# Graph attention over sorted edges on one core: three one-hot tables moved behind the spreads of q for the last tile, and the next queries' first part moved ahead of a node pair's add

## The chip, the cores and the metric

The kernel runs on one core of a Trainium2 chip. The metric is device microseconds of that core from start to end of one execution, median of several runs. Before the change it is 2704.53 us, the median of 3 runs between 2700.92 and 2709.87.

## What is computed

One layer of graph attention between two layer norms, on 12,500 nodes of 256 numbers and 200,000 edges. The edges come sorted by their destination `dst`; destinations are drawn as a square, so nodes with low numbers have far more edges than those with high ones. There are 8 heads of D = 32 numbers. The reference, cut to what matters:

```python
h = maximum(layernorm(x), 0)                      # (12500, 256)
q = (h @ Wq).reshape(n, 8, 32); k = h @ Wk; v = h @ Wv      # biases are zero
logits = einsum('ehd,ehd->eh', q[dst], k[src]) / sqrt(32)   # one row an edge
expv = exp(logits - segment_max(logits, dst)[dst])
attn = expv / segment_sum(expv, dst)[dst]
agg = segment_sum(attn[:, :, None] * v[src], dst)
out = agg.reshape(n, 256) + h @ Wskip
y = h + gelu(out)
return x + layernorm(y) * gamma + beta
```

## The kernel before

A first phase (to about 300 us) computes h, writes one table of keys and values to HBM (`kv_tab`, 512 floats a node: 256 of k, 256 of v) and lays out the edges. Then `walk_streams` goes through them. The edges are cut into S = 8 streams of consecutive edges. The walk makes NST = 66 steps (loop variable c); in a step each stream moves on by K = 3 tiles (j = 0, 1, 2) of 128 edges. A tile is thus 128 edges of 8 streams at once, with an edge on each partition.

What a tile goes through, with the name of the helper and its line:

- GpSimd (POOL) gathers the rows of `kv_tab` for the tile's sources with indirect DMAs (L1340), eight a tile, one for each stream, 24 a step. They land in the tile `kv`.
- TensorE spreads the queries: the q of a window of nodes (`qw`) times a one-hot table (`to_e`) gives each edge the q of its destination. `spread` (L1385 to L1396, the matmuls L1392) does half of the streams in a call and writes a PSUM tile `ps_qe`, of which there are two.
- VectorE multiplies the gathered keys by the spread q in `times` (L1402, again in two halves) and sums over each head in `total` (L1409).
- `turn` (L1428, TensorE; copy by ScalarE L1431) transposes the logits. Once a step, `maxima` takes running maxima over equal destinations (scans on VectorE, L1440 on; exp on ScalarE), and `turn_back` (L1450) transposes the weights back.
- `weigh` (L1477) multiplies the gathered values by the weights on VectorE, and `add_up` (L1500) sums them to their nodes: a matmul with another one-hot table (`to_n`). Its third call in a step is copied out by ScalarE (L1513).

The tables for a coming step are made ahead, two steps before they are used. `turn_windows` transposes the nodes' h (L1302, copy to `hwT` by ScalarE L1306), `queries` makes q of it (bias L1316, matmuls L1320, copy to `qw` by ScalarE L1323), in a first part of one block and a second of two. `hot_e` makes a block of the one-hot table `to_e`: a matmul (L1366) and a relu by ScalarE (L1369), four blocks a step. `hot_n` (L1379, L1382) makes `to_n`. These all take their PSUM from `ps_hot`, of which there are two.

The sums of finished nodes go to a table in HBM. From step 18 on, a `Pair` is finished in each step: two blocks of 128 nodes. Its parts run over three steps. `fetch` (six loads on SP's queue), then in the next step `turn` (L1071, copied by ScalarE L1074), `divisors`, `skip` (h @ Wskip, L1088), `divide` (L1077), `add` (L1093, adds the attention's result to the skip's in PSUM by an identity matmul for each block), `gelu` (ScalarE, L1097), and at the end of the step `stats` (VectorE, L1100 to L1109) and `root` (ScalarE, L1113); then, a step later, `factors` (VectorE, L1117 and L1118), `normal` (ScalarE, L1123), `shifted` (TensorE, L1153), `scale` (L1157) and `store` (SP, L1168). In the loop, `pair` is the one in its second step, `before` the one in its third and `pair_next` the one being fetched. In the stretch that is changed a `pair` is there in steps 19 to 63 (45 of them) and none in steps 0 to 18.

The order of the work is the order of the code. `keep` ties each instruction to the one before it on the same engine, so TensorE, VectorE, ScalarE and SP run them exactly as the loop calls them. The gathers have their own rule: a list `waiting` holds the rows that may be gathered next (a tile's eight come in when its buffer was last read by `weigh`), and after each step of TensorE, `turns(latest[PE])` takes one from the list and makes it wait for that matmul. A gather is thus paced by TensorE's order. GpSimd runs nothing else in these steps.

ScalarE changes its table of functions by `table_of` (L1262), which runs a dummy activation of one number: to Gelu ahead of `divide`, to Sqrt ahead of `root`, to Exp behind it.

The changed stretch is L1691 to L1713 of the main loop.

Of the kernel before, what the change touches and what calls it, by code (L numbers as in the profile page):

```python
# [48 lines left out]
S = 8  # L49
# [937 lines left out]
def walk_streams(tc, N, HID, NST, KL, many, ident, idx, d0_row, slot_row, near, near_n, e_tab, pen_tab, h_tab,  # L987
# [240 lines left out]
    with ExitStack() as es:  # L1228
# [132 lines left out]
        def hot_e(c, i):  # L1361

            if i == 0:
                step[c]["to_e"] = hot.tile([P, S // 2, CH], F32, name="to_e")
            ps = hot_ps.tile([P, S * WN], F32, name="ps_hot")
            keep(nc.tensor.matmul(ps[:, :CH], near[:, i * P:(i + 1) * P], step[c]["et"],  # L1366
                                  start=True, stop=True))
            turns(latest[PE])
            keep(nc.scalar.activation(step[c]["to_e"][:, i, :], ps[:, :CH], AF.Relu, scale=-1.0,  # L1369
                                      bias=ones))  # L1370
# [14 lines left out]
        def spread(c, j, half):  # L1385

            g = step[c]
            ps = qe_ps.tile([P, 2, 2, HID], F32, name="ps_qe")
            for a in range(2):
                for b in range(2):  # L1390
                    r = slice(b * WN, (b + 1) * WN)
                    keep(nc.tensor.matmul(ps[:, b, a, :],  # L1392
                                          g["to_e"][r, 2 * half + a, j * P:(j + 1) * P],
                                          g["qw"][r, (half + a) * half, :], start=True, stop=True))
            g["qe", half] = ps
            turns(latest[PE])  # L1396
# [220 lines left out]
        for c in range(NST - 1):  # L1617
# [73 lines left out]
            if pair:  # L1691
                table_of(AF.Gelu)
                pair.divide()
            if pair_next:
                pair_next.fetch()
            if before:
                before.store(1)
            if pair:
                pair.add()
            if c + 2 < NST:  # L1700
                queries(c + 2, 0)
            if pair:
                pair.gelu()
            turn(c + 1, 0)
            if c + 2 < NST:
                turn_windows(c + 2, 1)
                hot_e(c + 2, 0)
                queries(c + 2, 1)
                for i in range(1, S // 2):
                    hot_e(c + 2, i)  # L1710
            for half in range(2):
                times(c + 1, 1, half)
                spread(c + 1, K - 1, half)  # L1713
            total(c + 1, 1)
            weigh(c, 1)
            gather_next(c, 1)
# [491 lines left out]
```

## Time and profile before

| | |
|---|---|
| median of 3 runs | 2704.53 us |
| the profiled execution | 2724.49 us |
| its span in the trace | 2722.4 us |
| mean granted clock of TensorE | 0.815 |
| busy TensorE (PE) | 1982.6 us, 73% |
| busy VectorE (DVE) | 1869.3 us, 69% |
| busy GpSimd (POOL) | 1620.4 us, 60% |
| busy ScalarE (ACT) | 1100.8 us, 40% |
| moved by DMA | 596.02 MB, mean 219 GB/s |

The profiled execution took 20 us more than the median. Rows of the trace have the start and the duration in us, the engine, the line, the operation, out<-in with partitions x elements, and in brackets the engine's idle time ahead of it and what ended it. PE is TensorE, DVE VectorE, ACT ScalarE, POOL GpSimd, SP the queue that issues the plain DMAs. A releaser called "remote" is one that the profile can't name. Rows of a timeline that stand for several instructions give the first one's start and the time that all took together.

### The profile page before, as it was taken

What the parts mean: (1) busy time and instruction counts of PE and PEld (TensorE: products, weight loads), DVE (VectorE), ACT (ScalarE), POOL (GpSimd) and SP (SyncE); (2) the same over time, 40 slices, a digit from 0 to 9 for tenths busy, and PEclk for the clock granted to TensorE, in tenths of its full rate; (3) what the DMA queues carried; (4) which work ended last, traced back from release to release, by engine and by line L of the source; (5) the groups of instructions that cost most, each with busy time, mean ns of one, the idle gap of its engine ahead of it and who ended that gap; (6) DMA issues with size and microseconds to landing.
All of it is one profiled execution on the core that took longest, in us unless ns stands there. A gap on an engine that the chain in (4) does not pass through costs nothing.

```text
span 2722.4 us, 36232 instructions
## 1 busy us (share of the span) xinstructions
PE 1982.6 (73%) x10159; PEld 1181.6 (43%) x10159; DVE 1869.3 (69%) x2165; ACT 1100.8 (40%) x2576; POOL 1620.4 (60%) x1741
## 2 busy tenths in 40 slices
PE   9994567677677677677766777777777777777776
PEld 4442344344444444444444444444444444444443
DVE  8872666666666667766767677776677767776776
ACT  5741222222222244444444444444444444444444
POOL 5456566666666665666556556656656666565652
PEclk9996777877777788888888887888888888888878
DMA  9786566777676777777777777777777777777773
GB/s 348 287 292 196 170 200 203 208 211 206 202 206 204 217 224 217 210 220 228 221 215 213 220 220 221 219 224 225 231 218 219 220 221 229 217 216 213 230 210 108
DMA packets 278904, 596.02 MB, mean 219 GB/s; under 512 B 53040, under 2 KB 166852, under 8 KB 275616
## 3 DMA queue, kind: packets, MB, share of 16 engines
q0 software_dynamic: 128224, 421.39, 53.5%
q1 hardware_dynamic: 148996, 170.91, 19.4%
q8 instruction: 83, 1.36, 0.2%
q10 hardware_dynamic: 1472, 1.31, 0.2%
q14 instruction: 129, 1.06, 0.1%
HBM read 510.92 MB, written 82.47 MB: 218 GB/s over the span
## 4 chain that ended last, share of the span: by engine, by line
PE 43%; another core or an unknown queue 14%; issue 13%; DVE 12%; ACT 11%; POOL 3%; DMA 2%; SPq 2%; DVEq 0%; POOLq 0%; ACTq 0%
PE ps_qe L1392 9%; PE ps_a L1088 6%; PE ps_a L1500 5%; PE ps_hot L1320 5%; ACT kv L1517 4%; DVE vw L1477 4%; PE ps_kv L340 4%; DVE kv L1402 3%; DVE L L1409 2%; PE ps_hot L1500 2%; POOL kv L1340 2%; ACT sums_w L1513 2%; ACT to_n L1382 2%; PE ps_hot L1153 2%
## 5 line engine op out<-in xcount | busy, mean ns | idle before, releaser
L1340 POOL DMA_INDIRECT kv<-kv_tab,idx x1520 | 1454.5, 957 | 926.3 <-issue 370.1
L1402 DVE TENSOR_TENSOR kv<-ps_qe,kv 128x1024 f32<-128x1024 f32 x392 | 466.6, 1219 | 587.5 <-remote 266.2
L1392 PE MATMUL ps_qe<-qw,to_e 64*128 64x256 f32 x3136 | 526.1, 476 | 216.2 <-issue 116.4
L1477 DVE TENSOR_TENSOR vw<-ps_x,kv 128x2048 f32<-128x2048 f32 x194 | 442.0, 2278 | 151.2 <-ACT vw L1466 123.7
L1392 PEld LDWEIGHTS ps_qe<-qw,to_e 64*128 64x128 f32 x3136 | 384.6, 234 | 370.8 <-issue 259.0
L1409 DVE TENSOR_REDUCE L<-kv 128x64 f32<-128x2048 f32 x196 | 447.7, 2284 | 5.1
L1323 ACT COPY qw<-ps_hot 128x256 f32<-128x256 f32 (+1 forms) x132 | 63.2, 479 | 601.6 <-PE ps_hot L1320 322.3
L1320 PE MATMUL ps_hot<-w_q,hwT 128*128 128x256 f32 x792 | 246.9, 456 | 19.2 <-ACT hwT L1306 18.8
L1500 PE MATMUL ps_a<-vw,to_n 128*32 128x264 f32 (+1 forms) x2304 | 237.0, 433 | 23.4 <-ACT kv L1517 18.3
L1320 PEld LDWEIGHTS ps_hot<-w_q,hwT 128*128 128x128 f32 x792 | 164.5, 222 | 117.7 <-issue 70.1
L1306 ACT COPY hwT<-ps_hot 128x256 f32<-128x256 f32 (+1 forms) x132 | 63.3, 480 | 360.4 <-PE ps_hot L1302 189.7
L340 PE MATMUL ps_kv<-w_kv,hT 128*128 128x512 f32 x392 | 184.5, 594 | 1.0 <-ACT hT L254 0.7
L1262 ACT ACT_TABLE_LOAD x139 | 178.3, 1283 | 2.6
L1088 PE MATMUL ps_a<-w_s,hT 128*128 128x256 f32 x360 | 167.7, 645 | 11.2 <-issue 4.8
L1379 PE MATMUL ps_hot<-near_n,et 48*128 48x384 bf16 x196 | 63.0, 376 | 143.3 <-ACT to_n L1382 139.3
L1366 PE MATMUL ps_hot<-et,near 48*128 48x384 bf16 x264 | 93.0, 353 | 91.7 <-ACT ps_x L1431 44.8
L1369 ACT ACTIVATE to_e<-ps_hot,ones 128x384 f32<-128x384 f32 x264 | 142.8, 581 | 10.4 <-PE ps_hot L1366 8.6
L1500 PEld LDWEIGHTS ps_a<-vw,to_n 128*32 128x32 f32 (+1 forms) x2304 | 95.2, 127 | 112.6 <-ACT kv L1517 39.6
L1517 ACT COPY kv<-ps_a 1x264 f32<-1x264 f32 x384 | 141.5, 368 | 6.3
L1088 PEld LDWEIGHTS ps_a<-w_s,hT 128*128 128x128 f32 x360 | 112.5, 328 | 58.7 <-issue 29.7
L1123 ACT ACTIVATE sums<-sums,nm,rstd 128x256 f32<-128x256 f32 x90 | 49.1, 592 | 211.0 <-DVE nm L1118 120.5
L1513 ACT COPY sums_w<-ps_a 128x264 f32<-128x264 f32 x128 | 48.4, 378 | 202.1 <-remote 74.7
(327 smaller groups left out, 2334.6 us busy)
## 6 DMA issues: line engine op xcount, KB each, us to landing
kv<-kv_tab,idx POOLq DMA_INDIRECT x1568
kv_tab<-kvo SPq DMA_DIRECT2D x23, 1024.0 KB
hw<-h_tab SPq DMA_DIRECT2D x264, 64.0 KB
table<-sums_w SPq DMA_DIRECT2D x260, 61.9 KB
pen<-pen_tab SPq DMA_DIRECT2D x66, 192.5 KB
sums<-table SPq DMA_DIRECT2D x92, 132.0 KB
x_in<-in_x_dram SPq DMA_DIRECT2D x23, 512.0 KB
h_tab<-h SPq DMA_DIRECT2D x23, 512.0 KB
```

The source lines that it names most:

```text
L340: nc.tensor.matmul(ps_kv, hT[:, c, :], w_kv[:, c, :], start=c == 0, stop=c == KC - 1)
L1088: self.keep(nc.tensor.matmul(self.ps[:, b, :], self.hT[:, b, c, :], w_s[:, c, :], start=False, stop=False, skip_group_check=True))
L1262: keep(nc.scalar.activation(dummy[:, 1:2], dummy[:, 0:1], function))
L1320: keep(nc.tensor.matmul(ps[:, b, :], g["hwT"][:, b, k, :], w_q[:, k, :], start=False, stop=k == KC - 1, skip_group_check=True))
L1340: ins = nc.gpsimd.indirect_dma_start(out=t[:, s, :], out_offset=None, in_=kv_tab[:, :], in_offset=bass.IndirectOffsetOnAxis(ap=idx[:, s, j ...
L1369: keep(nc.scalar.activation(step[c]["to_e"][:, i, :], ps[:, :CH], AF.Relu, scale=-1.0, bias=ones))
L1392: keep(nc.tensor.matmul(ps[:, b, a, :], g["to_e"][r, 2 * half + a, j * P:(j + 1) * P], g["qw"][r, (half + a) * half, :], start=True, stop= ...
L1402: keep(nc.vector.tensor_tensor(k, g["qe", half].rearrange("p b a d -> p a b d"), k, op=OP.mult))
L1409: keep(nc.vector.tensor_reduce(g["L"][:, j, :].rearrange("p (s h) -> p s h", s=S), g["kv"][j][:, :, :HID].rearrange("p s (h d) -> p s h d" ...
L1477: keep(engine.tensor_tensor(t[:, :, HEADS:].rearrange("p s (h d) -> p s h d", h=HEADS), wj[:, :, :, None].to_broadcast([P, t.shape[1], HEA ...
L1500: keep(nc.tensor.matmul(ps[at:at + w, :], g["to_n"][:, j, i * P + at:i * P + at + w], g["vw"][j][:, s, :], start=j == 0, stop=j == tiles_o ...
L1517: keep(copy(step[c + 1]["kv"][0][0:1, s, HID - HEADS:], ps[at:at + 1, :]))
```

## The change

Only the order of calls within one step of the walk changes; no call is added or taken away.

```diff
--- before.py
+++ after.py
@@ -1691,26 +1691,27 @@
             if pair:
                 table_of(AF.Gelu)
                 pair.divide()
+            if before:
+                before.store(1)
             if pair_next:
                 pair_next.fetch()
-            if before:
-                before.store(1)
-            if pair:
-                pair.add()
             if c + 2 < NST:
                 queries(c + 2, 0)
             if pair:
-                pair.gelu()
+                pair.add()
             turn(c + 1, 0)
             if c + 2 < NST:
                 turn_windows(c + 2, 1)
                 hot_e(c + 2, 0)
                 queries(c + 2, 1)
-                for i in range(1, S // 2):
-                    hot_e(c + 2, i)
+            if pair:
+                pair.gelu()
             for half in range(2):
                 times(c + 1, 1, half)
                 spread(c + 1, K - 1, half)
+            if c + 2 < NST:
+                for i in range(1, S // 2):
+                    hot_e(c + 2, i)
             total(c + 1, 1)
             weigh(c, 1)
             gather_next(c, 1)
```

On TensorE, ahead of the changed calls stand the spreads of the second tile (L1392). Then the pair's add (L1093) and the first part of the queries (L1316, L1320) change places. Before:

```order
L1392 MATMUL ps_qe<-qw,to_e 128x256 x8
L1093 MATMUL ps_a<-o,ident 128x256 x2
L1316 LDWEIGHTS one_row
L1316 MATMUL ps_hot<-b_q_70,one_row 128x256
L1320 MATMUL ps_hot<-w_q,hwT 128x256 x2
L1428 MATMUL ps_x<-ident,L 64x128
L1302 MATMUL ps_hot<-ident,hw 128x128 x4
```

With the change:

```order
L1392 MATMUL ps_qe<-qw,to_e 128x256 x8
L1316 LDWEIGHTS one_row
L1316 MATMUL ps_hot<-b_q_70,one_row 128x256
L1320 MATMUL ps_hot<-w_q,hwT 128x256 x2
L1093 MATMUL ps_a<-o,ident 128x256 x2
L1428 MATMUL ps_x<-ident,L 64x128
L1302 MATMUL ps_hot<-ident,hw 128x128 x4
```

The add now stands between the first part of the queries and the transpose of the logits (L1428).

A little further on TensorE, behind the queries' second part, stand the one-hot tables (L1366) and the spreads of the step's last tile. Before:

```order
L1320 MATMUL ps_hot_12845<-w_q_68,hwT_12838 128x256 x4
L1366 LDWEIGHTS near_84
L1366 MATMUL ps_hot_12853<-et_12592,near_84 128x384
L1366 LDWEIGHTS near_84
L1366 MATMUL ps_hot_12857<-et_12592,near_84 128x384
L1366 LDWEIGHTS near_84
L1366 MATMUL ps_hot_12861<-et_12592,near_84 128x384
L1392 MATMUL ps_qe_12865<-qw_12519,to_e_12538 128x256 x4
L1392 MATMUL ps_qe_12871<-qw_12519,to_e_12538 128x256 x4
L1428 MATMUL ps_x_2267<-ident_62,L_12790 64x128
```

With the change:

```order
L1320 MATMUL ps_hot_12844<-w_q_68,hwT_12837 128x256 x4
L1392 MATMUL ps_qe_12854<-qw_12517,to_e_12537 128x256 x4
L1392 MATMUL ps_qe_12861<-qw_12517,to_e_12537 128x256 x4
L1366 LDWEIGHTS near_84
L1366 MATMUL ps_hot_12867<-et_12592,near_84 128x384
L1366 LDWEIGHTS near_84
L1366 MATMUL ps_hot_12870<-et_12592,near_84 128x384
L1366 LDWEIGHTS near_84
L1366 MATMUL ps_hot_12873<-et_12592,near_84 128x384
L1428 MATMUL ps_x_2267<-ident_62,L_12790 64x128
```

Both halves of the spread now stand ahead of the three tables. Since each of these calls takes one waiting gather, the seventh and eighth gather of the tile in turn, which were tied to the first two of these three tables, are now tied to the two halves of the spread. GpSimd's own order is the same, and so is VectorE's.

On ScalarE the pair's gelu (L1097) moves. Before, from the load of the Gelu table to the relu of the last three one-hot blocks:

```order
L1262 ACTIVATE dummy<-dummy 1x1
L1323 COPY qw<-ps_hot 128x256
L1097 ACTIVATE sums<-ps_a 128x512
L1431 COPY ps_x<-M 64x1
L1306 COPY hwT<-ps_hot 128x512
L1369 ACTIVATE to_e<-ps_hot,ones 128x384
L1323 COPY qw<-ps_hot 128x512
L1369 ACTIVATE to_e<-ps_hot,ones 128x384 x3
```

With the change:

```order
L1262 ACTIVATE dummy<-dummy 1x1
L1323 COPY qw<-ps_hot 128x256
L1431 COPY ps_x<-M 64x1
L1306 COPY hwT<-ps_hot 128x512
L1369 ACTIVATE to_e<-ps_hot,ones 128x384
L1323 COPY qw<-ps_hot 128x512
L1097 ACTIVATE sums<-ps_a 128x512
L1369 ACTIVATE to_e<-ps_hot,ones 128x384 x3
```

The gelu now stands behind the copies of the transposed logits, of `hwT` and of the queries' second part, and still ahead of the three relus, behind which come the load of the Sqrt table and the pair's root. On SP's queue, the store of the second block of `before` goes ahead of the six loads of `pair_next`.

## Prediction

> **What bounds the kernel now.** I read the page first, then the table of what VectorE waited for, then the timeline of one step. From the page, its first line and the chain that ended last by engine:
>
> ```profile
> span 2722.4 us, 36232 instructions
> PE 43%; another core or an unknown queue 14%; issue 13%; DVE 12%; ACT 11%; POOL 3%; DMA 2%; SPq 2%; DVEq 0%; POOLq 0%; ACTq 0%
> ```
>
> No engine fills the span, and 14% of the chain goes to releasers that the profile cannot name ("another core" cannot be: there is one). VectorE's waits (line, releaser, us in total, times, longest) say where:
>
> ```profile
> DVE kv L1402 <- remote: 266.2, 63, 34.2
> DVE kv L1402 <- PE ps_qe L1392: 208.6, 69, 9.0
> ```
>
> L1402 multiplies the gathered keys by the spread queries, L1392 is the spread. The dominant wait is thus for spreads, with half of it unnamed. The scan L1440 runs once a step, so it gives the step's length (start, duration):
>
> ```profile
> 991.90 0.95 DVE L1440 TENSOR_TENSOR_SCAN ps_x<-pen,ps_x 64x384 f32<-64x384 f32 x1
> ...
> 2626.68 0.95 DVE L1440 TENSOR_TENSOR_SCAN ps_x<-pen,ps_x 64x384 f32<-64x384 f32 x1
> ```
>
> These are the scans of steps 20 and 63, all with a node pair to finish: (2626.68 - 991.90)/43 = 38.0 us a step. By the code the reordered stretch runs with a pair in 45 steps (c = 19 to 63) and without one in 19 (c = 0 to 18). One step with a pair, four engines together, in order of time:
>
> ```profile
> 1046.57 1.13 PE L1093 MATMUL ps_a<-o,ident 128*128 128x256 f32 x4
> 1047.31 0.95 POOL L1340 DMA_INDIRECT kv<-kv_tab,idx  x1 [0.30 <-issue]
> 1049.24 0.94 POOL L1340 DMA_INDIRECT kv<-kv_tab,idx  x1 [0.98 <-PE ps_x L1428]
> 1049.28 0.60 ACT L1097 ACTIVATE sums<-ps_a 128x512 f32<-128x512 f32 x1
> 1049.85 0.59 ACT L1306 COPY hwT<-ps_hot 128x512 f32<-128x512 f32 x1
> 1050.49 0.37 PE L1316 MATMUL ps_hot<-b_q,one_row 3*128 3x512 bf16 x1 [0.70 <-ACT ps_x L1431]
> 1050.79 1.99 PE L1320 MATMUL ps_hot<-w_q,hwT 128*128 128x256 f32 x8
> 1052.61 0.68 DVE L1100 TENSOR_TENSOR sums<-sums,h 128x512 f32<-128x512 f32 x1
> 1053.30 1.57 ACT L1369 ACTIVATE to_e<-ps_hot,ones 128x384 f32<-128x384 f32 x3
> 1053.94 0.32 PE L1366 MATMUL ps_hot<-et,near 48*128 48x384 bf16 x1 [0.16 <-issue]
> 1053.95 2.04 PE L1392 MATMUL ps_qe<-qw,to_e 64*128 64x256 f32 x16
> 1054.42 0.95 POOL L1340 DMA_INDIRECT kv<-kv_tab,idx  x1 [0.30 <-issue]
> 1054.89 1.28 ACT L1262 ACT_TABLE_LOAD   x1
> 1056.30 0.28 ACT L1113 ACTIVATE rstd<-mv,eps 128x2 f32<-128x2 f32 x1
> 1058.18 0.95 POOL L1340 DMA_INDIRECT kv<-kv_tab,idx  x1 [0.31 <-issue]
> 1060.20 2.35 DVE L1402 TENSOR_TENSOR kv<-ps_qe,kv 128x1024 f32<-128x1024 f32 x2 [5.90 <-remote]
> 1061.28 0.94 POOL L1340 DMA_INDIRECT kv<-kv_tab,idx  x1 [2.16 <-remote]
> 1062.47 0.15 DVE L1117 RECIPROCAL rstd<-rstd 128x2 f32<-128x2 f32 x1
> ```
>
> VectorE idles 5.90 us before the last tile's multiplies at 1060.20, although TensorE's records put their spreads at 1053.95 to 1055.99. So TensorE's answer reaches VectorE more than 4 us after its record ends, and GpSimd's next gather (1061.28) waits for TensorE too, unnamed as well. What holds the answer? GpSimd issued gathers back to back from 1049.24 to 1058.18 + 0.95 = 1059.13, and the answer came 1.07 us after it had run out of gathers that may start. A second place in the step looks the same: ScalarE waits for the last add_up.
>
> ```profile
> 1072.70 0.95 POOL L1340 DMA_INDIRECT kv<-kv_tab,idx  x1 [0.30 <-issue]
> 1074.74 0.38 ACT L1513 COPY sums_w<-ps_a 128x264 f32<-128x264 f32 x1 [3.13 <-remote]
> ```
>
> Here the answer comes 1.09 us after the last gather's 1073.65. And one step in which GpSimd paused by chance for 2.12 us just before the spreads:
>
> ```profile
> 2154.47 0.94 POOL L1340 DMA_INDIRECT kv<-kv_tab,idx  x1 [2.12 <-issue]
> 2157.48 1.23 DVE L1402 TENSOR_TENSOR kv<-ps_qe,kv 128x1024 f32<-128x1024 f32 x1 [1.02 <-PE ps_qe L1392]
> ```
>
> There the first multiply waited only 1.02 us, with the spread named as its releaser. My reading: a long run of gathers holds back TensorE's answers. It rests on coincidence in time, so the rivals keep weight.
>
> **The change part by part.** Nothing is added or removed; VectorE's and GpSimd's orders stay.
>
> TensorE: the next queries' first part goes ahead of the older pair's add (1.06 us from 1046.57), so its answer comes about 1.06 us sooner. ScalarE: the gelu (0.60 at 1049.28) leaves its place ahead of the hwT copy, which can begin some 0.3 us sooner; the queries' second part waited 0.70 us for that copy, so it ends near 1052.4, not 1052.78. Three one-hot tables (the last is the row at 1053.94) no longer stand ahead of the spreads: these begin near 1052.4 instead of 1053.95, **1.55 us sooner**, and by their record (2.04 for both halves) the first half is done at 1053.4.
>
> Gathers: each is tied to a step of TensorE's order, one per call. Gathers 7 and 8 of the next step's first tile were tied to one-hot tables 1 and 2; they are now tied to the two halves of the spread. GpSimd's run starts 0.68 us sooner (the gather after 1047.31 may follow at 48.56, not 49.24), its sixth gather (1054.42) ends at 55.37 - 0.68 = 54.7, and the seventh may not start before the first half is answered. If the run holds the answer, the run now ends itself: answer at 54.7 + 1.07 = 55.8 instead of 1060.2.
>
> What is late next is ScalarE. Tables 1 to 3 now stand behind the spreads, and ScalarE's relu of them, the Sqrt table load and the older pair's root behind those: relu 0.58, table 3's matmul 0.32 (two banks), relus to 1.71, load 1.28, the dummy 0.13 (from the load's end, 1056.17, to the root at 1056.30), root 0.28, about 3.5 us after the answer. VectorE's reciprocal (L1117) waits for the root in order. At 55.8 + 3.5 = 59.3 it stands 3.2 us ahead of 1062.47. If instead the first half is answered at once and only the second held, one gather later (1.25), it is 60.5: 1.95 sooner. I take the middle, **2.6 us a step**: 45 x 2.6 = 117 us.
>
> The gelu behind the queries' second copy makes VectorE's stats (1052.61) about 1 us later, ending near 55.4; that lies in the 5.90 us of idle time and costs nothing unless the answer is at 53.4, when it sets the multiplies' start. The store of the finished pair's second block goes ahead of the six fetches on SP: one issue of 0.36 us from the row
>
> ```profile
> 1046.72 0.36 SPq L1168 DMA_DIRECT2D out_dram<-o  x1
> ```
>
> The fetched rows are used a step later, so I take 0; bounds -16 to +16 us (45 x 0.36).
>
> Steps without a pair:
>
> ```profile
> 691.93 1.23 DVE L1402 TENSOR_TENSOR kv<-ps_qe,kv 128x1024 f32<-128x1024 f32 x1 [2.40 <-PE ps_qe L1392]
> 696.20 1.23 DVE L1402 TENSOR_TENSOR kv<-ps_qe,kv 128x1024 f32<-128x1024 f32 x1 [3.04 <-PE ps_qe L1392]
> 696.46 0.94 POOL L1340 DMA_INDIRECT kv<-kv_tab,idx  x1 [1.98 <-PE ps_qe L1392]
> ```
>
> Only the second half is held. Its hold could shrink by all of 3.04 us, but GpSimd is back at the next tile at about 695.8 instead of 696.46, and the later holds follow GpSimd. Between 0 and 3.0 I take 0.7, GpSimd's row: 19 x 0.7 = 13 us.
>
> Sum: 117 + 13 = **130 us** less. The profiled execution took 2724.49 us (span 2722.4), 20 us above the median of the runs, 2704.53. Taken from the median: **2575 us**.
>
> **The clock, and a rule that says more.** The other wait of each step, ahead of the next tile's spreads, has the pair's skip matmuls in it, and these run slowly. First an idle time and the matmuls behind it, with the clock share (third number from the end) there and where the queries ran; then a step with less idle time:
>
> ```profile
> 1038.88 0.47 PE L1379 MATMUL ps_hot<-near_n,et 48*128 48x384 bf16 x1 [4.04 <-ACT to_n L1382]
> 1041.14 3.57 PE L1088 MATMUL ps_a<-w_s,hT 128*128 128x256 f32 x8
> ```
> ```profile
> 1040.00:1042.00 2.00, 1.86 (x6) 0.94 (x5) 1.67 (x1) 1.78 (x5) 1.70 (x2) 0.50 0.85 261
> 1050.00:1052.00 2.00, 1.51 (x7) 1.08 (x7) 2.00 (x2) 0.91 (x2) 1.39 (x3) 1.00 0.93 264
> ```
> ```profile
> 1689.86 0.48 PE L1379 MATMUL ps_hot<-near_n,et 48*128 48x384 bf16 x1 [0.94 <-ACT to_n L1382]
> 1692.12 3.78 PE L1088 MATMUL ps_a<-w_s,hT 128*128 128x256 f32 x8
> ```
>
> Eight records of this shape take 3.57 us at a share of 0.50 and 1.99 at 1.00 (L1320, 1050.79). Were the share 1.00 here, 1.6 us a step would go. The row at 1692.12 speaks against it: a single idle time of 0.94 did not bring it back. I leave it out of the sum and price it as a rival. The Trainium skill (TensorE: Matmul & The Clock Gate, "Part 1: The HAM clock gate") says that an idle window of about 3.4 us halves the clock and as much busy time restores it; by that rule 4.04 us of idle time lies just above the border, and a hold shorter by 0.7 us would bring the full clock.
>
> **The rivals.**
> - *The hold is not GpSimd's and ends when it does now (slower).* Then the answer stays at 1060.2, and tables 1 to 3, which were done before the hold, stand in it. The root comes at 60.2 + 3.5 = 63.7, and VectorE's reciprocal, 62.47 now, waits 1.2 us in every step with a pair: +54 us, **2759**. It turns slower from an answer later than 59.0. For it: at 1060.20 and 1074.74 many things end together. Against it: the pause at 2154.47.
> - *The hold has a fixed length behind its spread (small gain).* Answer at 60.2 - 1.55 = 58.65, reciprocal at 62.15: 0.3 x 45 = 14 us, and up to 1.3 x 19 = 25 where no root follows: 2665 to 2690, **2680**. This is also the case in which the change does nothing that can be told from noise.
> - *The hold goes altogether (larger gain).* Multiplies at 55.4, reciprocal near 58.3: 4.2 x 45 + 3.0 x 19 = 246 us, **2459**.
> - *The forecast, and the clock stays up behind the other hold.* 117 + 13 + 1.6 x 45 = 202 us, **2503**. Only if the earlier answers shorten that idle time too.
>
> **How the numbers follow.** Forecast 2575: 0.42. Slower rival: 0.28. Fixed hold: 0.20, of which 0.12 above a gain of 0.3% and 0.08 within (0.3%, 8 us, is about what a measurement tells from no change). Hold gone: 0.05. Clock up: 0.05. Both signs are likely: the forecast's own range runs from 2704.5 - 45 x 3.2 - 19 x 3.0 = 2504 to 2704.5 - 45 x 1.95 = 2617. The whole range reaches the slower rival with 5 us around it: 2504 to 2764. Faster 0.64, same 0.08, slower 0.28.
>
> **What would show it.** Right: the idle time before the last tile's first multiply falls from 5.9 to about 2 us, the reciprocal (L1117 in the old numbering) waits for the root, GpSimd shows a gap before its seventh gather, and steps with a pair take about 35.4 us. Wrong: that idle time stays near 5 to 6 us and the reciprocal waits over 1 us behind it (slower rival), or the steps keep 38 us because the second hold, before the copy of the last sums, grows by what the first one lost.

## The result and the profile after

The changed kernel takes 2719.03 us (median of 7 runs, 2713.68 to 2721.82), the kernel before 2704.53 (7 runs, 2697.60 to 2709.87): a ratio of 1.0058, 95% interval 1.0044 to 1.0071. It is 0.6% **slower**, where 2575 was forecast. The profiled execution took 2720.00 us, 1 us from its median; that of the kernel before, 2724.49, stood 20 us above its own. So the two traces put the changed kernel 4.5 us ahead, where the medians put it 14.5 behind: the traces can show where waits moved, but their totals can't stand for the loss.

The page, first line and chain by engine:

```profile
span 2717.9 us, 36189 instructions
PE 38%; another core or an unknown queue 15%; DVE 14%; issue 14%; ACT 13%; POOL 2%; DMA 2%; SPq 1%; POOLq 0%; DVEq 0%; ACTq 0%
```

The unnamed part is about as large as it was (14%). VectorE's waits (line, releaser, us in total, times, longest), of the changed kernel and then one row of the kernel before:

```profile
DVE vw L1477 <- ACT vw L1466: 243.9, 61, 7.2
DVE kv L1402 <- PE ps_qe L1392: 180.6, 52, 6.9
DVE kv L1402 <- remote: 103.5, 33, 29.8
DVE sums L1100 <- issue: 76.8, 34, 3.3
...
DVE sums L1100 <- ACT qw L1323: 23.1, 8, 3.4
DVE rstd L1117 <- issue: 17.2, 14, 2.5
```
```profile
DVE vw L1477 <- ACT vw L1466: 123.7, 52, 5.8
```

The wait for spreads fell: its two rows from 266.2 + 208.6 = 474.8 us to 284.1, 191 less. But the wait ahead of the weighing of the first tile (L1477) grew by 120, and about 117 us in these rows stand in places where VectorE did not wait before: ahead of the pair's stats (L1100, 76.8 + 23.1) and of the reciprocal (L1117, 17.2). These are the largest rows only. All of VectorE's idle time in the steps with a pair, added up from the rows of each trace over the 44 steps from the first pair's to the last pair's, in us a step (`e2_gelu_back_3`, the change without the gelu's move, is described below):

| VectorE idle ahead of | before | after | `e2_gelu_back_3` |
|---|---|---|---|
| the last tile's multiplies (L1402) | 5.84 | 0.86 | 0.98 |
| the pair's stats (L1100) | 0 | 2.36 | 0 |
| the reciprocal (L1117) | 0 | 0.67 | 1.68 |
| the weighing of the first tile (L1477) | 1.96 | 3.18 | 4.54 |
| the second tile's multiplies (L1402) | 2.90 | 3.35 | 3.04 |
| everything | 11.06 | 10.78 | 10.61 |

**The wait that the change went for is nearly gone, and almost all of it stands elsewhere.** The two scans that were used for the step:

```profile
990.99 0.95 DVE L1440 TENSOR_TENSOR_SCAN ps_x<-pen,ps_x 64x384 f32<-64x384 f32 x1
...
2624.84 0.95 DVE L1440 TENSOR_TENSOR_SCAN ps_x<-pen,ps_x 64x384 f32<-64x384 f32 x1
```

(2624.84 - 990.99)/43 = 38.0 us a step, as before. In the steps without a pair, the scans of steps 1 and 18, first before, then after the change:

```profile
310.72 0.96 DVE L1440 TENSOR_TENSOR_SCAN ps_x<-pen,ps_x 64x384 f32<-64x384 f32 x1 [0.52 <-PE ps_x L1428]
...
916.80 0.96 DVE L1440 TENSOR_TENSOR_SCAN ps_x<-pen,ps_x 64x384 f32<-64x384 f32 x1 [0.39 <-PE ps_x L1428]
```
```profile
305.75 0.96 DVE L1440 TENSOR_TENSOR_SCAN ps_x<-pen,ps_x 64x384 f32<-64x384 f32 x1 [1.89 <-PE ps_x L1428]
...
917.27 0.96 DVE L1440 TENSOR_TENSOR_SCAN ps_x<-pen,ps_x 64x384 f32<-64x384 f32 x1 [1.99 <-PE ps_a L1500]
```

That is 606.1 us before and 611.5 after: these 17 steps got 5.4 us longer, 0.3 a step, where 0.7 a step less was forecast. One step of the changed kernel, in order of time:

```profile
1045.79 2.35 DVE L1402 TENSOR_TENSOR kv<-ps_qe,kv 128x1024 f32<-128x1024 f32 x2 [3.16 <-PE ps_qe L1392]
...
1050.25 1.99 PE L1320 MATMUL ps_hot<-w_q,hwT 128*128 128x256 f32 x8
...
1052.30 0.95 POOL L1340 DMA_INDIRECT kv<-kv_tab,idx  x1 [0.31 <-issue]
...
1054.53 0.58 ACT L1323 COPY qw<-ps_hot 128x512 f32<-128x512 f32 x1 [4.15 <-PE ps_hot L1366]
1054.77 0.95 POOL L1340 DMA_INDIRECT kv<-kv_tab,idx  x1 [1.52 <-PE ps_hot L1366]
1055.02 0.60 ACT L1097 ACTIVATE sums<-ps_a 128x512 f32<-128x512 f32 x1
...
1055.65 0.69 DVE L1100 TENSOR_TENSOR sums<-sums,h 128x512 f32<-128x512 f32 x1 [2.99 <-issue]
...
1056.03 1.14 POOL L1340 DMA_INDIRECT kv<-kv_tab,idx  x1 [0.30 <-issue]
...
1057.37 2.36 DVE L1402 TENSOR_TENSOR kv<-ps_qe,kv 128x1024 f32<-128x1024 f32 x2
...
1059.64 0.16 DVE L1117 RECIPROCAL rstd<-rstd 128x2 f32<-128x2 f32 x1
...
1065.70 0.95 DVE L1440 TENSOR_TENSOR_SCAN ps_x<-pen,ps_x 64x384 f32<-64x384 f32 x1
...
1071.49 0.38 ACT L1513 COPY sums_w<-ps_hot 128x264 f32<-128x264 f32 x1 [4.27 <-remote]
...
1076.92 2.29 DVE L1477 TENSOR_TENSOR vw<-ps_x,kv 128x2048 f32<-128x2048 f32 x1 [3.71 <-ACT vw L1466]
...
1083.22 2.36 DVE L1402 TENSOR_TENSOR kv<-ps_qe,kv 128x1024 f32<-128x1024 f32 x2 [3.27 <-PE ps_qe L1392]
```

By chance this step begins at the same time as the one that the prediction shows: 1045.79 against 1045.82. So the two can be laid side by side. The kernel before goes on from there like this:

```profile
1045.82 2.35 DVE L1402 TENSOR_TENSOR kv<-ps_qe,kv 128x1024 f32<-128x1024 f32 x2 [2.47 <-PE ps_qe L1392]
...
1068.53 0.95 DVE L1440 TENSOR_TENSOR_SCAN ps_x<-pen,ps_x 64x384 f32<-64x384 f32 x1
...
1077.89 2.29 DVE L1477 TENSOR_TENSOR vw<-ps_x,kv 128x2048 f32<-128x2048 f32 x1 [1.87 <-ACT vw L1466]
...
1083.37 2.35 DVE L1402 TENSOR_TENSOR kv<-ps_qe,kv 128x1024 f32<-128x1024 f32 x2 [2.46 <-PE ps_qe L1392]
```

The last tile's multiplies come 2.83 us sooner (1057.37 against 1060.20), the reciprocal 2.83 (1059.64 against 1062.47), the scan 2.83 (1065.70 against 1068.53). Then the second copy of the sums (from `ps_hot`) waits 4.27 us, where in the kernel before it was the third (from `ps_a`) that waited, 3.13; the weighing is only 0.97 us sooner, and the next step's multiplies 0.15. So in this step the gain was there in the middle, and was given back before the end. Over the 44 steps, VectorE's idle time from the stats to the reciprocal shrank by 5.84 - 0.86 - 2.36 - 0.67 = 1.95 us a step, less than the 2.6 of the forecast, and the two waits behind took 1.22 + 0.45 of it.

### The profile page after: what moved, and what is told of

Read it like the earlier page. It is cut to its first block, busy times and chain, and to the rows that moved or that the text cites. A ratio compares the mean times of both kernels' runs of the same rounds, so it can differ in the third digit from the quotient of the medians.

```text
span 2717.9 us, 36189 instructions
## 1 busy us (share of the span) xinstructions
PE 1927.9 (71%) x10159; PEld 1165.6 (43%) x10159; DVE 1873.5 (69%) x2165; ACT 1111.0 (41%) x2576; POOL 1621.1 (60%) x1741
## 4 chain that ended last, share of the span: by engine, by line
PE 38%; another core or an unknown queue 15%; DVE 14%; issue 14%; ACT 13%; POOL 2%; DMA 2%; SPq 1%; POOLq 0%; DVEq 0%; ACTq 0%
PE ps_qe L1392 9%; PE ps_a L1088 6%; ACT kv L1517 6%; DVE vw L1477 5%; PE ps_hot L1320 5%; PE ps_kv L340 4%; DVE L L1409 3%; PE ps_a L1500 3%; ACT sums_w L1513 2%; DVE kv L1402 2%; PE ps_hot L1071 2%; ACT to_n L1382 2%; PE ps_hot L1379 1%; POOL kv L1340 1%
## 5 line engine op out<-in xcount | busy, mean ns | idle before, releaser
L1402 DVE TENSOR_TENSOR kv<-ps_qe,kv 128x1024 f32<-128x1024 f32 x392 | 462.9, 1218 | 337.6 <-PE ps_qe L1392 180.6
L1477 DVE TENSOR_TENSOR vw<-ps_x,kv 128x2048 f32<-128x2048 f32 x194 | 442.1, 2279 | 255.4 <-ACT vw L1466 243.9
L1392 PE MATMUL ps_qe<-qw,to_e 64*128 64x256 f32 x3136 | 511.7, 476 | 19.2 <-issue 17.4
L1392 PEld LDWEIGHTS ps_qe<-qw,to_e 64*128 64x128 f32 x3136 | 377.7, 241 | 209.3 <-issue 150.5
L1320 PE MATMUL ps_hot<-w_q,hwT 128*128 128x256 f32 x792 | 244.9, 453 | 18.5 <-ACT hwT L1306 18.2
L1366 PE MATMUL ps_hot<-et,near 48*128 48x384 bf16 x264 | 81.4, 331 | 204.4 <-issue 127.6
L1320 PEld LDWEIGHTS ps_hot<-w_q,hwT 128*128 128x128 f32 x792 | 163.5, 221 | 123.2 <-issue 76.2
L1450 PE MATMUL ps_x<-ident,W 64*128 64x64 f32 x195 | 34.4, 304 | 239.5 <-issue 143.6
L1088 PE MATMUL ps_a<-w_s,hT 128*128 128x256 f32 x360 | 170.1, 654 | 12.8 <-ACT hT L1074 6.7
L1379 PE MATMUL ps_hot<-near_n,et 48*128 48x384 bf16 x196 | 79.8, 471 | 100.2 <-ACT to_n L1382 87.8
L1088 PEld LDWEIGHTS ps_a<-w_s,hT 128*128 128x128 f32 x360 | 113.7, 331 | 59.7 <-issue 24.7
L1450 PEld LDWEIGHTS ps_x<-ident,W 64*128 64x128 f32 x195 | 23.1, 187 | 269.9 <-issue 161.4
```

Source lines behind the costliest of these rows:

```text
L1088: self.keep(nc.tensor.matmul(self.ps[:, b, :], self.hT[:, b, c, :], w_s[:, c, :], start=False, stop=False, skip_group_check=True))
L1320: keep(nc.tensor.matmul(ps[:, b, :], g["hwT"][:, b, k, :], w_q[:, k, :], start=False, stop=k == KC - 1, skip_group_check=True))
L1392: keep(nc.tensor.matmul(ps[:, b, a, :], g["to_e"][r, 2 * half + a, j * P:(j + 1) * P], g["qw"][r, (half + a) * half, :], start=True, stop= ...
L1402: keep(nc.vector.tensor_tensor(k, g["qe", half].rearrange("p b a d -> p a b d"), k, op=OP.mult))
L1477: keep(engine.tensor_tensor(t[:, :, HEADS:].rearrange("p s (h d) -> p s h d", h=HEADS), wj[:, :, :, None].to_broadcast([P, t.shape[1], HEA ...
```

## The experiments

The runs were made in five sessions, each on one chip, and these are of two kinds. In two of them the kernel before took 2702.72 and 2730.17 us, about as in the first measurement; in the three others 2242.71, 2242.39 and 2241.55, 17% less, with the same program. So each kernel is compared with the kernel before in its own session. I call the first kind sessions with holds, since only there TensorE's answers come late; the expectations speak of chips with and without holds. But the kind does not go with the chip as far as it was recorded: the first session (2242.71) and the last (2730.17) were both on the chip with number 15. Whether that is one chip or the same number in two machines isn't known.

The theories, as the expectations name them: **A**, runs of gathers hold TensorE's answers until GpSimd runs dry. **B**, the gelu's new place made the loss. **C**, where nothing is held, 24 gathers set the step. **D**, the loss belongs to the holds. **E**, the reordering helps VectorE nowhere. **F**, a break in the run only moves the hold to the next piece of work.

**What the faster sessions look like.** `before_again` and `after_again` are the two kernels unaltered.

> The changed kernel unaltered, because the first four runs landed on a chip on which the kernel before takes 2242.71 us, not 2704.53. On that chip GpSimd issued gathers almost without a break and no answer of TensorE was held. Theory C (where no answer is held, the step is as long as its 24 gathers, 24 x 1.255 = 30.1 us, and the change can only lose, by the root and the reciprocal that stand behind tables 1 to 3): 0.3 to 1.0% slower than the kernel before on the same chip, near 2255. Theory D (the loss of 0.58% belongs to the held answers): no difference where nothing is held, 2238 to 2248; and again 0.6% slower where the kernel before takes 2700.

> The kernel before unaltered, for its trace on this chip. Ratio 1.000 to itself within 0.3%. If no answer of TensorE is held: VectorE's idle time ahead of the last tile's multiplies is under 1 us a step instead of 5.41, and a step with a pair takes 29.8 to 30.2 us.

`before_again` took 2242.41 us (ratio 0.9998, 0.9988 to 1.0008), `after_again` 2240.94 against 2242.39 (0.9992, 0.9982 to 1.0002): there the change makes **no difference**. Theory C expected a loss of 0.3 to 1.0% and is wrong in that. D is right for a session without holds; its other half, the loss again where there are holds, was not run a second time. From the timeline of `before_again`, GpSimd's gathers and VectorE around the last tile's multiplies:

```profile
1016.60 0.95 POOL L1340 DMA_INDIRECT kv<-kv_tab,idx  x1 [0.30 <-PE ps_x L1428]
...
1017.85 0.95 POOL L1340 DMA_INDIRECT kv<-kv_tab,idx  x1 [0.30 <-ACT hwT L1306]
1019.10 0.95 POOL L1340 DMA_INDIRECT kv<-kv_tab,idx  x1 [0.30 <-DMA kv<-kv_tab,idx]
...
1020.35 1.08 POOL L1340 DMA_INDIRECT kv<-kv_tab,idx  x1 [0.30 <-PE ps_hot L1320]
...
1021.74 0.95 POOL L1340 DMA_INDIRECT kv<-kv_tab,idx  x1 [0.30 <-PE ps_hot L1366]
1022.60 2.36 DVE L1402 TENSOR_TENSOR kv<-ps_qe,kv 128x1024 f32<-128x1024 f32 x2 [0.97 <-DMA kv<-kv_tab,idx]
1022.99 0.95 POOL L1340 DMA_INDIRECT kv<-kv_tab,idx  x1 [0.30 <-issue]
```

GpSimd never stops, and the multiplies wait for a gather, not for a spread. My rule that a run of gathers holds the answers cannot be a rule of the gathers alone: here the run never ends and nothing is held. The group of gathers on the page (count, busy and mean ns, idle ahead of them), of `before_again`, then of the kernel before and the changed kernel in the first measurement, with holds:

```profile
L1340 POOL DMA_INDIRECT kv<-kv_tab,idx x1520 | 1453.4, 956 | 463.3 <-issue 228.0 <-DMA kv<-kv_tab,idx 105.4 <-PE ps_qe L1392 25.3
```
```profile
L1340 POOL DMA_INDIRECT kv<-kv_tab,idx x1520 | 1454.5, 957 | 926.3 <-issue 370.1 <-PE ps_qe L1392 196.6 <-remote 162.8
```
```profile
L1340 POOL DMA_INDIRECT kv<-kv_tab,idx x1520 | 1454.8, 957 | 920.5 <-issue 342.6 <-PE ps_qe L1392 216.2 <-remote 153.3
```

In the faster session a gather costs (1453.4 + 463.3)/1520 = 1.261 us with its pause, and 24 of them 30.3 us. The step is as long:

```profile
849.57 0.96 DVE L1440 TENSOR_TENSOR_SCAN ps_x<-pen,ps_x 64x384 f32<-64x384 f32 x1
...
2155.04 0.95 DVE L1440 TENSOR_TENSOR_SCAN ps_x<-pen,ps_x 64x384 f32<-64x384 f32 x1
```

(2155.04 - 849.57)/43 = 30.4 us, a little over the 29.8 to 30.2 that were expected; the idle time ahead of the last tile's multiplies is 2.10 us a step, 0.80 of it ahead of the first half, where under 1 was expected. With holds the gathers themselves take the same time, but GpSimd stands idle 926.3 - 463.3 = 463 us more, and 457 us more with the change. VectorE's busy time is alike too (1867.6 and 1869.3 us); TensorE's is not (1782.1 and 1982.6 us, at a mean granted clock of 0.900 and 0.815).

**A break in the run of gathers.** The kernel before, with tiny memsets on GpSimd ahead of one gather in each step with a pair (each gather is tied behind the instruction ahead of it on GpSimd, so that the memsets stay at their place):

```diff
+        def pause():
+            for _ in range(8):
+                ins = nc.gpsimd.memset(rest_t, 0.0)
+                behind(ins, last["pool"])
+                last["pool"] = ins.ins.name
...
                 hot_e(c + 2, 0)
+                if pair:
+                    pause()
                 queries(c + 2, 1)
```

> The kernel before with eight tiny memsets on GpSimd (about 2 to 2.8 us together) in each of the 45 steps with a pair, ahead of the gather that goes with the queries' second part. Where answers are held and theory A is right (the hold ends when GpSimd runs dry), the pause lets the spreads of the last tile be answered on time: VectorE's 5.4 us of idle time there shrink by 2 or more a step, up to 100 us less, about 2620 on a chip with 2704. Where nothing is held and theory C is right (24 gathers set the step), each pause is paid in full: 45 x 2 to 2.8 = 90 to 126 us more, 2330 to 2370 on a chip with 2243. If neither holds, within 10 us of the kernel before.

> The kernel before with GpSimd's pause (1.74 us, eight memsets) ahead of the gather that goes with the queries' second part, for a chip with holds (kernel before near 2703). Theory A (the hold ends when GpSimd runs dry): the spreads of the last tile are answered in the pause, VectorE's 5.4 us there fall by 2 or more a step, 2600 to 2650. Theory F (the later gathers are only shifted, and the next hold grows by what this one lost): 2690 to 2720. On a chip without holds (before near 2242): 2330 again, as 45 x 1.94 us.

> The changed kernel with the same pause on GpSimd. On a chip with holds, theory A: the pause splits the run of six gathers ahead of the queries' second copy, whose answer came 2.3 us late; the gelu and the stats come on time, and the change shows what was forecast of it: 40 us or more below the kernel before with the pause. Theory F: equal to the kernel before with the pause within 15 us. On a chip without holds: 2330, as the kernel before with the pause.

> The kernel before with GpSimd's pause of 1.74 us. With holds (kernel before near 2703): 2600 to 2650 if the hold ends when GpSimd runs dry, 2690 to 2720 if the next hold grows by as much, more if it adds up. Without holds: 2330.

`p_pause` and `p_pause_2` fell in sessions without holds: 2329.56 against 2242.39 (1.0391, 1.0377 to 1.0405) and 2331.01 against 2241.55 (1.0402, 1.0388 to 1.0416); `p_pause_after`, the changed kernel with the pause, 2330.89 (1.0399, 1.0385 to 1.0413), beside 2241.55 too. That is (2329.56 - 2242.39)/45 = 1.94 us a step for a pause of 1.74: there GpSimd's time **is** the step, shown by lengthening it.

`p_pause_3` fell in a session with holds: 2845.64 against 2730.17 (1.0421, 1.0403 to 1.0439), slower by 115 us, 2.57 a step. Its timeline:

```profile
1062.07 1.75 POOL L1342 MEMSET rest_t<- 1x96 f32 x8
...
1063.16 2.36 DVE L1414 TENSOR_TENSOR kv<-ps_qe,kv 128x1024 f32<-128x1024 f32 x2 [0.90 <-DMA kv<-kv_tab,idx]
...
1064.36 0.95 POOL L1349 DMA_INDIRECT kv<-kv_tab,idx  x1 [0.53 <-PE ps_x L1440]
...
1074.44 0.95 POOL L1349 DMA_INDIRECT kv<-kv_tab,idx  x1 [0.31 <-issue]
1075.86 0.37 ACT L1306 COPY hwT<-ps_hot 128x256 f32<-128x256 f32 x1 [8.82 <-remote]
...
1077.33 0.96 DVE L1452 TENSOR_TENSOR_SCAN ps_x<-pen,ps_x 64x384 f32<-64x384 f32 x1 [3.60 <-remote]
```

The pause does what theory A says at its place: the spreads are answered, and the last tile's multiplies (now L1414) wait 0.90 us, and for a gather; over the 44 steps their idle time is 0.99 us instead of 5.84. But the gathers behind it now run without a break from 1064.36 to 1075.39, ScalarE's copy waits 8.82 us for an answer that comes 0.47 us after that run, and the scan, which has no wait in the rows of the kernel before, waits 3.60. The weighing of the first tile waits 5.43 us a step instead of 1.96. Theory A is right at the place where the pause stands and wrong on the time; F, that the next hold grows by as much, is nearer, and even short.

**Fewer gathers.** The rows of two of the eight streams are loaded by SP from fixed rows of the table, so GpSimd has 18 gathers a step; the output isn't the layer's.

```diff
         def gather_row(t, c, j, s, behind):
+            if s >= S - 2:
+                keep(nc.sync.dma_start(t[:, s, :], kv_tab[j * P:(j + 1) * P, :]))
+                return
```

> The kernel before with GpSimd relieved: the rows of streams 6 and 7 are not gathered but loaded by SP from fixed rows of the table (other edges' keys and values, so the output is not the layer's), 18 gathers a step instead of 24, the bytes alike. Theory C (on a chip where no answer is held, 24 gathers x 1.255 = 30.1 us set the step): with 18 x 1.255 = 22.6 us GpSimd is off the path and VectorE's work (26.7 us busy a step) with its waits for spreads becomes the limit: 27.5 to 29 us a step, 2110 to 2190 in all. If the gathers do not set the step: within 20 us of the kernel before.

> The changed kernel with GpSimd relieved in the same way (18 gathers a step, two streams from fixed rows). Theory C: now that GpSimd does not set the step, the earlier spreads show: VectorE's 0.8 us ahead of the last tile's multiplies go, the stats' new wait for the late gelu (0.63 us) stays: between 0 and 35 us under the relieved kernel before. Theory E (the reordering never helps VectorE, even when it is the limit, because gelu, root and tables come late by as much): equal to the relieved kernel before within 7 us, or slower.

> The kernel before with 18 gathers a step and two streams from fixed rows. With holds: 2376 again. Without holds, if 24 x 1.255 us set the step there: VectorE becomes the limit, 27.5 to 29 us a step with a pair, 2110 to 2190; if the gathers do not set it: 2230 to 2250.

> The changed kernel with 18 gathers a step. With holds: 0.4% under its partner again. Without holds: 0 to 35 us under its partner if the earlier spreads show as soon as GpSimd is off the path; equal within 7 us or slower if gelu, root and tables come late by as much.

Both pairs fell in sessions with holds. First pair: 2376.38 and 2367.63 against 2702.72 (0.8806, 0.8770 to 0.8842, and 0.8767, 0.8743 to 0.8790). Second: 2420.16 and 2375.83 against 2730.17 (0.8874, 0.8853 to 0.8895, and 0.8703, 0.8689 to 0.8718). So a quarter of the gathers away took 326 and 310 us off, although by the page GpSimd had 926 us of idle time to spare. Its idle time did not shrink with it (`g6_before`):

```profile
L1343 POOL DMA_INDIRECT kv<-kv_tab,idx x1140 | 1094.9, 960 | 938.3 <-issue 311.8 <-PE ps_x L1431 224.3 <-PE ps_a L1503 107.4
```

The gathers' own part of the 326 us would be 380 x 1.261 = 479, so other work shares the limit here. With GpSimd relieved the change shows a gain: 0.4% in the first pair (the intervals overlap), 1.8% in the second (they don't). Theory E is refuted by the second pair alone. The same two programs thus differ by 0.4% in one session with holds and by 1.8% in another, so a ratio found in one can't be set against a ratio found in another. No such pair was run without holds, so theory C's 2110 to 2190 was not tried.

**Which part of the change loses.** The spreads moved alone, `e1_spreads_only`, against the kernel before:

```diff
-                for i in range(1, S // 2):
-                    hot_e(c + 2, i)
             for half in range(2):
                 times(c + 1, 1, half)
                 spread(c + 1, K - 1, half)
+            if c + 2 < NST:
+                for i in range(1, S // 2):
+                    hot_e(c + 2, i)
```

The gelu back behind the add, `e2_gelu_back`, against the changed kernel:

```diff
                 pair.add()
+                pair.gelu()
             turn(c + 1, 0)
...
-            if pair:
-                pair.gelu()
```

The two small swaps alone, `e3_small_swaps`, against the kernel before:

```diff
+            if before:
+                before.store(1)
             if pair_next:
                 pair_next.fetch()
-            if before:
-                before.store(1)
-            if pair:
-                pair.add()
             if c + 2 < NST:
                 queries(c + 2, 0)
             if pair:
+                pair.add()
                 pair.gelu()
```

The gelu's move alone, `e4_gelu_only`, against the kernel before:

```diff
                 queries(c + 2, 0)
-            if pair:
-                pair.gelu()
             turn(c + 1, 0)
...
                 queries(c + 2, 1)
+                if pair:
+                    pair.gelu()
                 for i in range(1, S // 2):
                     hot_e(c + 2, i)
```

> The kernel before with one part of the change alone: the two spreads of the last tile stand ahead of one-hot tables 1 to 3; gelu, add, queries and store stay where they were. Theory A (runs of gathers hold TensorE's answers, and what is saved at one hold is given back at the next, since the next run of gathers starts later against the rest): VectorE's idle time ahead of the last tile's multiplies falls by about half, that ahead of the weighing of the first tile (L1477) grows by 1 us a step, and the time is 2695 to 2725. Theory B (the change lost its gain only because the gelu, and with it the stats, stand behind the queries' late copy: 103.7 + 29.7 us of new idle time ahead of stats and reciprocal): without the gelu's move the idle time ahead of the stats is gone and the time is near 2600.

> The changed kernel with the gelu alone back behind the add, ahead of the hwT copy. Theory A: the idle time of 2.43 us a step ahead of the stats (L1100) goes and comes back ahead of the last tile's multiplies (L1402) or of L1477; the time stays between 2695 and 2725. Theory B: 2.4 us x 45 = 108 us less than the changed kernel, about 2610.

> The kernel before with the two small parts alone: the queries' first part ahead of the add, and the finished pair's store ahead of the six fetches; gelu and spreads stay (the gelu right behind the add). Both theories: within 8 us of the kernel before, 2697 to 2713. If the small swaps carry the loss, 2715 to 2725.

> The kernel before with one part alone: the gelu behind the copy of the queries' second part, ahead of the relus of one-hot tables 1 to 3. The stats then wait for it in time in which VectorE waited for the spreads anyway (5.41 us a step on the mean). Theory A: 2697 to 2715, no change. Theory B: also no change, as the multiplies still wait for the late answer, unless the hold falls on the queries' copy here too; then up to 2720.

All four fell in a session without holds, where the kernel before takes 2242.71: 2258.12 (1.0071, 1.0058 to 1.0084), 2245.36 (1.0009, 0.9999 to 1.0020), 2243.30 (1.0003, 0.9995 to 1.0012) and 2242.87 (0.9994, 0.9985 to 1.0003). Only the spreads alone lose. One row of VectorE's waits there, and the same of `after_again`:

```profile
DVE rstd L1117 <- ACT rstd L1113: 41.7, 31, 1.8
```
```profile
DVE rstd L1117 <- ACT rstd L1113: 2.5, 13, 0.2
```

That is the slower rival's mechanism, in small: with the spreads alone ahead, the relus of tables 1 to 3 end so late that the root holds up the reciprocal. With the two small swaps as well (`e2_gelu_back`) the loss is gone, so the parts belong together. That it is the queries' first part that brings all this about 1 us sooner is argued: it was not tried without the store's swap. Theory B's 2600 was for sessions with holds and could not be tried here.

`e5_tables_late` is the changed kernel with the gelu back behind the add (as in `e2_gelu_back`), and with the three tables behind the root, at the end of the step:

```diff
                 spread(c + 1, K - 1, half)
-            if c + 2 < NST:
-                for i in range(1, S // 2):
-                    hot_e(c + 2, i)
             total(c + 1, 1)
...
                 pair.root()
                 table_of(AF.Exp)
+            if c + 2 < NST:
+                for i in range(1, S // 2):
+                    hot_e(c + 2, i)
```

> The changed kernel with the gelu back behind the add and with one-hot tables 1 to 3 at the end of the step, behind the pair's root and the load of the Exp table, so that the root waits for no relu. Theory C: the reciprocal's idle time (0.31 us a step in the kernel with the gelu back, 1.03 with the spreads moved alone) goes; the time is that of the kernel before within 5 us, not less, since the gathers set the step. If the next step's first spread waits for the late tables instead, 0.5% or more slower.

2244.47 against 2242.39 (1.0010, 1.0001 to 1.0019): no gain, as expected where the gathers set the step.

Two of these kernels again, for a session with holds:

> The spreads moved alone, again, for a chip with holds. If the gelu's place carries the loss (103.7 us of new idle time ahead of the stats): near 2600 to 2680, faster than the kernel before. If what one hold loses the next gains: 2700 to 2725. On a chip without holds: 0.7% slower, as in the first run.

> The changed kernel with the gelu back behind the add, again, for a chip with holds. If the gelu's place carries the loss: faster than the kernel before by 1% or more (below 2675). If what one hold loses the next gains: 2695 to 2725. On a chip without holds: equal to the kernel before, as in the first run.

> The changed kernel with the gelu back behind the add. With holds: below 2675 if the gelu's place carried the loss, 2695 to 2725 if what one hold loses the next gains. Without holds: equal to the kernel before within 0.2%.

`e1_spreads_only_2` and `e2_gelu_back_2` fell in a session without holds once more: 2261.03 (1.0087, 1.0074 to 1.0101) and 2243.58 (1.0012, 1.0003 to 1.0021) against 2241.55. `e2_gelu_back_3` fell in one with holds: 2724.11 against 2730.17, 0.9976 (0.9959 to 0.9993). So there the change without the gelu's move gains 0.2%, where the whole change lost 0.6% in the first measurement. That the 0.8% between them is the price of the gelu's place is not shown, since the whole change was not run beside it. It is not theory B's gain of 1% or more: the stats no longer wait, but by the table above VectorE's idle time is 10.61 us a step instead of 10.78. The reciprocal and the weighing of the first tile took it back, the latter from 123.7 us of waits in the kernel before to

```profile
DVE vw L1477 <- ACT vw L1466: 294.1, 61, 7.2
```

The steps without a pair hold no gelu, so they show the rest of the change alone. From the scan of step 1 to that of step 18, `p_pause_3`, which in these steps is the kernel before, took 606.9 us beside that run (311.90 to 918.77), and `e2_gelu_back_3`, which in them is the changed kernel, 617.5 (306.87 to 924.37). With the 606.1 and 611.5 of the first measurement, these steps lose 5 to 11 us with holds, by one trace of each.

No version of the change that was run beats the kernel before of its session by more than 0.3% with all 24 gathers.

## Why the prediction was wrong

- **The hold at the last tile's spreads would shrink: right, and by more than was said.** The idle time there was to fall from 5.9 to about 2 us; ahead of both multiplies it fell from 5.84 to 0.86 on the mean. In the step shown, the multiplies and the reciprocal came 2.83 us sooner, where 2.6 was taken. That the two agree is in part luck: the multiplies were to start at 55.8, at the answer, and the reciprocal to wait for the root until 59.3 or 60.5. They started at 57.37, behind the late stats, and the reciprocal came right behind them, with no wait in this step.
- **"VectorE's reciprocal (L1117) waits for the root in order": right in kind.** By the working it was to wait from 55.8 + 2.35 = 58.15 to 59.3, about 1.2 us a step; it waited 0.67 on the mean.
- **"The seventh may not start before the first half is answered": the run of gathers ended one earlier.** The gap of 1.52 us, the row at 1054.77, stands ahead of the tile's sixth gather, the one tied to the queries' second part; the seventh (1056.03) follows without one. Counted over the 45 steps with a pair, GpSimd stood idle more than 0.6 us ahead of the sixth gather in 27, of the eighth in 17 and of the seventh in 2, and in the kernel before in 0, 0 and 1. The working let the sixth gather run freely, so it took the queries' answer to be on time.
- **The gelu's move "costs nothing unless the answer is at 53.4": wrong.** The hold had moved from the spreads to the queries' second part: its matmuls end at 1052.24 and ScalarE is answered at 1054.53, 1.28 us after a run of six gathers (the last from 1052.30 to 1053.25). The gelu stood behind that copy, so the stats came 3.04 us later, not about 1, and set the start of the multiplies.
- **The failing step is the term 45 x 2.6 = 117 us:** VectorE's earlier start was taken for a shorter step. It is the case that the prediction named last under what would prove it wrong: other holds took back what the first one lost. Of the 4.98 us a step that went ahead of the last tile's multiplies, 2.36 came back ahead of the stats, 0.67 ahead of the reciprocal, 1.22 ahead of the weighing of the first tile and 0.45 ahead of the second tile's multiplies, and the steps with a pair kept their 38.0 us. The prediction read what releases the answers, GpSimd running dry, and did not ask what that makes of GpSimd: where the holds end on GpSimd's schedule, moving one piece of TensorE's work moves the hold on to another piece. `p_pause_3` and `e2_gelu_back_3` show the same: each takes one wait away, and the next ones grow.
- **The term 19 x 0.7 = 13 us has the wrong sign:** the steps without a pair got about 0.3 us longer each.
- **What bounds the kernel was misread.** Lengthening GpSimd's time moves the total in both kinds of session, and removing gathers moves it with holds, where alone that was run. Taking VectorE's largest wait away (`p_pause_3`) does not bring the time down, though GpSimd's time grew there too. The page showed GpSimd busy 60%, which hid that a gather also has a pause of about 0.3 us: 24 x 1.261 = 30.3 of the 38.0 us a step. I quoted that pause in every gather's row and never summed it.
- **The rivals.** The slower rival's time (2759) needed the spreads' answer to stay at 1060.2; in the step shown the multiplies began at 1057.37. A hold of fixed length behind the spread is refuted by `p_pause_3`, where a pause of GpSimd took it away. The clock rival's condition came in part and its gain did not: the wait ahead of L1379, on which it hung, went from 139.3 to 87.8 us (L1382 as releaser), but the skip's matmuls behind it (L1088) took 654 ns each on the mean instead of 645, and the mean granted clock went from 0.815 to 0.822 only.
- **Open.** Why TensorE's answers are held in some sessions while GpSimd issues gathers and not in others, with the same program, isn't settled, and chip number 15 is on both sides. Whether TensorE's lower clock with holds is a cause or a consequence wasn't tried either. That GpSimd running dry releases the answers is the best reading and not a rule: of 42 waits of over 2 us ahead of the last tile's first multiply that end with TensorE or an unnamed releaser in the trace of the kernel before, 32 end 0 to 2.0 us after a gather with none running, and 10 while a gather runs. Of the 14.5 us of loss, the steps without a pair may hold 5; where the rest sits is not known. The spreads alone were not measured with holds.

## What to carry to other kernels

Before a wait is priced as path, ask which engine decides when it ends, and sum that engine's time in a step with its issue pauses; an engine that the page shows 72% busy, as GpSimd in `before_again`, can be the limit. Test it by lengthening that engine's work a little: if the total follows in full, expect that shorter waits elsewhere are only moved. Add up an engine's idle time over all its places, before and after: a wait that is gone at one place says nothing until the sum has fallen. When work is put ahead of a late answer, look for what now stands behind the next late answer (here the gelu, and with it the stats).

## What the runs showed of the hardware

- The same program took 2242 us in three sessions and 2703 and 2730 in two others, with chip number 15 on both sides. The gathers' own duration is alike (956 and 957 ns), and so is VectorE's busy time; GpSimd stands idle 463 us more in the slower trace.
- In the slower sessions answers of TensorE mostly come after GpSimd's run of gathers has ended: 0.47 to 1.28 us after it in the rows shown (1075.39 to 1075.86; 1053.25 to 1054.53), up to 2.0 us ahead of the last tile's multiplies in the trace of the kernel before. Eight small memsets in the run (1.75 us) let the spreads' answer through as well. Six gathers fewer a step took 310 to 326 us off.
- A gather of 128 rows of 2 KB costs GpSimd 0.956 us and a pause of about 0.30 us ahead of the next, also where nothing else made it wait (the rows that end in `0.30 <-issue`).
